# Attention scores for the exponentials from stacks of bfloat16 levels, with the maximum as three more rows and two sets of stacks

## The chip, the cores and the metric

The kernel runs on one core of a Trainium2 chip. The metric is the device time of one execution in microseconds. Engines are called PE (the matrix engine, with PEld for its weight loads), DVE (vector), ACT (scalar), POOL (GpSimd) and SP (it issues DMAs here).

## The reference

Four layers on x of shape (8, 256, 32, 32) in float32: an attention block with an MLP, a deformable convolution bottleneck, a binary convolution and a DCNv3 block. The change lies in the attention, which for each of 8 images, with N = 1024 pixels and 16 heads of key width 16 and value width 64, computes

```python
y = _bn(xf, g1, b1)
q = (einsum('bcn,oc->bon', y, wq) + bq).reshape(B, NH, KD, N).transpose(0, 1, 3, 2)
k = (einsum('bcn,oc->bon', y, wk) + bk).reshape(B, NH, KD, N)
v = (einsum('bcn,oc->bon', y, wv) + bv).reshape(B, NH, D, N).transpose(0, 1, 3, 2)
attn = softmax(einsum('bhnk,bhkm->bhnm', q, k) / KD ** (-0.5), axis=-1)   # scores times 4
o = einsum('bhnm,bhmd->bhnd', attn, v).transpose(0, 1, 3, 2).reshape(B, NH * D, N)
xf = xf + einsum('bdn,od->bon', o, wp) + bp
```

## The kernel before

**Blocks and steps.** The attention is cut into 32 groups of four heads of one image, and each group into two halves of the queries (512 each): 64 blocks. A block has 8 steps, one for each 128 keys (`kt` 0 to 7); there are 512 steps in all, run as one pipeline by `step(t)`. The order of the instructions of PE, ACT, DVE and POOL is the order in which the program emits them; only SP's queue of DMAs is ordered by the framework.

**What a step does**, in this order:

- `exps` (L443) of the next step: for each of four heads a float32 matmul (L453) of 128 keys by 512 queries into an "sc" bank (four in rotation), then ACT's exponential (L454) into an `e` buffer that holds two heads (six in rotation). The matmul contracts 32 rows: 16 rows of k and q, a row that is 1 in `ks` and minus the query's maximum in `qs`, and zero rows. The four heads lie in four groups of 32 partitions.
- `found(0)`, `attend` of heads 0 and 1, `found(1)`, `attend` of heads 2 and 3, `found(2)`, then planned work in three places (0, 1, 2), then `found(3)`.

`found` calls `score_max` (L399), which looks for the maxima of a block AHEAD = 11 steps before its own step: two bfloat16 matmuls of 64 queries by 512 keys (L408, a pair of heads side by side) into a "pb" bank, and DVE's maximum over it (L412). There are two "pb" banks, and every projection, `total` and `add_projected` uses them in rotation too, so a matmul into one waits until DVE or ACT has read what it held two uses before.

The bfloat16 scores come from *stacks* `sq` and `sk`. q and k are each split in three bfloat16 levels (`split`: L359 subtracts the first level, ACT copies the second at L364, L366 leaves the third; DVE does the subtractions), written to DRAM (`lev_d`), and `stack` (L374) reads them back so that eight products of a level of q and a level of k lie on eight times 16 rows. There is one set of stacks; the next group's are loaded when this group's maxima are found. `spread` (L380) brings the float32 q and k, by way of `u_d` in DRAM, into `qs` and `ks`, of which there are two sets.

`enter_max` (L422), once a block, at `kt` = 5 of the block before it, place 0 (the block's first `exps` come at `kt` = 7): DVE clears and reduces (L430, L431), transposes four 32x32 squares (L434), and SP issues four DMAs (L441), one for each head, into the maximum's row of `qs`.

`attend` (L460) multiplies the exponentials with v (L465, two heads to a pair) and adds them up for the denominators: POOL adds 128x1024 float32 per pair of heads (L473 at `kt` = 1, L475 after), 14 a block. In the last block DVE takes half of them. The denominators are finished during the next block: `total` (PE L486, ACT L493) at its `kt` = 3, `narrow` (four DMAs, L499) at 4, `invert` (DVE, L502) at 6, `put` (L506) at 7, `lay` (four DMAs, L513) at 8, `scale` (POOL, L518, 128x512, twice) at 10 and 11, `add_projected` (PE L548, DVE L554 or L556) at 13 and 15.

Beside this, planned by group: `project_v` (L391) of the next group at four steps of the 16, `project_qk` (L333) for two groups at once in every second group (its steps 8, 9, 10 and 14), each followed by its splits, `stack` in 6 of the 16 steps, and `normed` on ACT. The prologue projects and splits for the first two groups (on POOL) and finds the first block's maxima in float32 (`score_max_first`) from `qs` and `ks`.

Of the kernel before, what the change touches and what calls it, by code (L numbers as in the profile page):

```python
# [8 lines left out]
F32 = mybir.dt.float32  # L9
# [19 lines left out]
DH, HID = NH * HD, 1024  # L29

# [128 lines left out]
def conv_seq_kernel(ctx: ExitStack, tc: tile.TileContext, d: dict, out: bass.AP):  # L159
# [76 lines left out]
    with ExitStack() as s0:  # L236
# [10 lines left out]
        row16 = w.tile([P, 1], F32, name="row16")  # L247
        nc.vector.tensor_add(row16, ident[:, 16:17], ident[:, 48:49])
        nc.vector.tensor_add(row16, row16, ident[:, 80:81])
        nc.vector.tensor_add(row16, row16, ident[:, 112:113])  # L250
        qs = [w.tile([P, N], F32, name=f"q{i}") for i in range(2)]
        ks = [w.tile([P, N], F32, name=f"k{i}") for i in range(2)]
        for i in range(2):
            nc.gpsimd.memset(qs[i], 0.0)
            nc.vector.tensor_copy(ks[i], row16.to_broadcast([P, N]))
        sq, sk = ([w.tile([P, 2, N], BF16, name=f"s{n}{i}") for i in range(2)] for n in "qk")
        ones = w.tile([P, HD], F32, name="ones_a")
# [21 lines left out]
        taken = w.tile([P, 4, KD], F32, name="taken")  # L279
# [39 lines left out]
        parts, u_d, lev_d = {}, {}, {}  # L319
        QK = [(0, 0), (1, 0), (1, 1), (0, 1)]  # L320

        def project_qk(b, g2, i):

            if i == 0:
                u_d[b, g2] = ld.tile([2, P, N], F32, name="u_d")
                lev_d[b, g2] = ld.tile([2, 3, P, N], BF16, name="lev_d")
# [20 lines left out]
            nc.sync.dma_start(u_d[b, g2][which, :, cols], u)  # L347
# [21 lines left out]
        def stack(b, g, pair, i, engines=(nc.sync, nc.sync)):  # L369

            for which, dst, eng in ((0, sq[pair], engines[0]), (1, sk[pair], engines[1])):
                r0 = (g % 2) * 64 + pair * 32
                src = lev_d[b, g // 2][which, i % 3 if which else i // 3, r0 : r0 + 32, :]
                eng.dma_start(dst[i * KD : (i + 1) * KD, :, :], src.rearrange("(j r) c -> r j c", r=KD))  # L374

        def spread(b, g, j, eng=nc.sync):

            for u, dst in zip((u_d[b, g // 2][0], u_d[b, g // 2][1]), (qs[g % 2], ks[g % 2])):
                r0 = (g % 2) * 64 + j * KD
                eng.dma_start(dst[32 * j : 32 * j + KD, :], u[r0 : r0 + KD, :])  # L380
# [16 lines left out]
        maxima = {}  # L397

        def score_max(m, s, i):  # L399
# [7 lines left out]
            for c in range(2):  # L407
                nc.tensor.matmul(  # L408
                    ps[c * 64 : (c + 1) * 64, :], sq[pair][:, c, q0 : q0 + 64],
                    sk[pair][:, c, kh * HALF : (kh + 1) * HALF], start=True, stop=True,  # L410
# [3 lines left out]
        def score_max_first(m, s, j):  # L414

            if m not in maxima:
# [5 lines left out]
                ps, qs[0][r, qt * P : (qt + 1) * P], ks[0][r, kh * HALF : (kh + 1) * HALF], start=True, stop=True  # L422
# [3 lines left out]
        def enter_max(m):  # L426

            b, g, h = m
            nm = sp.tile([P, 32], F32, name="nm")
            nc.vector.memset(nm[:, 16:32], 0.0)  # L430
            nc.vector.tensor_reduce(nm[:, 0:16], maxima.pop(m).rearrange("p a b k -> p (a b) k"), AX.X, ALU.max, negate=True)  # L431
            line = sp.tile([32, P], F32, name="line", bufs=1)
            for i in range(4):
                nc.vector.transpose(line[:, 32 * i : 32 * (i + 1)], nm[32 * i : 32 * (i + 1), :])  # L434
            for j in range(4):
                row = qs[g % 2][32 * j + KD : 32 * j + KD + 1, h * HALF : (h + 1) * HALF]
                if m == blocks[0]:
                    src = line[4 * j : 4 * j + 4, :]
                else:
                    src = line[j // 2 * 8 : j // 2 * 8 + 8, j % 2 * 64 : j % 2 * 64 + 64]  # L440
                nc.sync.dma_start(row.rearrange("o (q p) -> o q p", p=src.shape[1]), src)  # L441
# [3 lines left out]
        def exps(m, kt, j):  # L445

            b, g, h = m
            q, k = qs[g % 2], ks[g % 2]
# [3 lines left out]
            r = slice(32 * j, 32 * j + 32)  # L452
# [1432 lines left out]
```

## Time and profile before

| | |
|---|---|
| time, median of 3 executions | 4497.62 us (4492.69 to 4501.10) |
| profiled execution: span | 4474.0 us (its own time beside the span is not given) |
| the three executions less that span | 18.7 to 27.1 us |
| PE busy | 4012.0 us, 90% |
| POOL busy | 3317.7 us, 74% |
| DVE busy | 2858.2 us, 64% |
| ACT busy | 1876.2 us, 42% |
| L412, maxima on DVE | 2016 instructions, 688 ns mean |
| L475 and L473, adds on POOL | 762 and 127, 2423 and 2406 ns mean |
| L453, L465, L408 on PE | 590.7, 1048.4 and 765.7 us busy |
| L359 and L366, splits on DVE | 60 each, 1505 and 1231 ns mean |

The span runs from the first instruction to the last. The page divides it into 40 equal slices and gives a busy share in tenths for each engine and slice; PEclk is the clock that PE was granted, in tenths of full speed. The attention takes slices 1 to 23. Groups of instructions are listed as line, engine, operation, output<-inputs, shape and count; a line of a timeline begins with its start in microseconds and its duration, and ends with the idle time of its engine before it and what ended that. Matmuls are pipelined, so the busy time of a line with several can hold more than the distance of their starts; distances are taken from starts.

### The profile page before, as it was taken

What the parts mean: (1) busy time and instruction counts of PE and PEld (TensorE: products, weight loads), DVE (VectorE), ACT (ScalarE), POOL (GpSimd) and SP (SyncE); (2) the same over time, 40 slices, a digit from 0 to 9 for tenths busy, and PEclk for the clock granted to TensorE, in tenths of its full rate; (3) what the DMA queues carried; (4) which work ended last, traced back from release to release, by engine and by line L of the source; (5) the groups of instructions that cost most, each with busy time, mean ns of one, the idle gap of its engine ahead of it and who ended that gap; (6) DMA issues with size and microseconds to landing.
All of it is one profiled execution on the core that took longest, in us unless ns stands there. A gap on an engine that the chain in (4) does not pass through costs nothing.

```text
span 4474.0 us, 59867 instructions
## 1 busy us (share of the span) xinstructions
PE 4012.0 (90%) x20901; PEld 1525.3 (34%) x20901; DVE 2858.2 (64%) x4976; ACT 1876.2 (42%) x3366; POOL 3317.7 (74%) x2019
## 2 busy tenths in 40 slices
PE   6999999999999999999999998677767766999877
PEld 3333333333333333333333333233223322444332
DVE  5666666666666666666667663455445545688885
ACT  2555555555555555555555542122212212534331
POOL 3889989889889988898888963455454553078887
PEclk8999999999999999999999998888888888999988
DMA  5222222222222222122222112222232332100000
GB/s 165 67 66 55 63 76 57 62 69 60 62 72 57 57 69 70 52 65 74 60 62 69 49 50 60 78 85 85 77 97 67 91 112 63 38 10 15 15 19 21
DMA packets 224279, 284.12 MB, mean 64 GB/s; under 512 B 104400, under 2 KB 134624, under 8 KB 223712
## 3 DMA queue, kind: packets, MB, share of 16 engines
q1 hardware_dynamic: 193408, 196.49, 15.5%
q0 software_dynamic: 28720, 77.90, 5.9%
q10 hardware_dynamic: 1840, 5.81, 0.3%
q8 instruction: 168, 2.75, 0.3%
q14 instruction: 143, 1.17, 0.1%
HBM read 214.10 MB, written 64.34 MB: 62 GB/s over the span
## 4 chain that ended last, share of the span: by engine, by line
PE 74%; DVE 8%; another core or an unknown queue 6%; POOL 5%; issue 4%; ACT 1%; DMA 1%; ACTq 0%; DVEq 0%; SPq 0%; POOLq 0%
PE av L465 19%; PE sc L453 12%; PE pb L408 11%; PE pb L391 5%; PE pb L548 5%; PE pc L1305 3%; PE pm L779 3%; PE po L792 3%; PE pb L333 2%; POOL part L1504 2%; DVE near_p L956 2%; PE pc L1027 1%; DVE samp L960 1%; PE pw L1478 1%
## 5 line engine op out<-in xcount | busy, mean ns | idle before, releaser
L412 DVE TENSOR_REDUCE pm<-pb 128x1 f32<-128x512 f32 x2016 | 1373.7, 688 | 765.7 <-PE pb L408 762.1
L475 POOL TENSOR_TENSOR esum<-esum,e 128x1024 f32<-128x1024 f32 x762 | 1821.0, 2423 | 49.6 <-ACT e L454 49.0
L454 ACT ACTIVATE e<-sc 128x512 f32<-128x512 f32 x2048 | 1056.9, 602 | 593.3 <-PE sc L453 586.9
L465 PE MATMUL av<-e,v 128*64 128x512 f32 x4096 | 1048.4, 592 | 0.0
L934 POOL DMA_INDIRECT g<-table,idx x576 | 549.8, 955 | 560.6 <-DVE near_p L956 287.6
L408 PE MATMUL pb<-sk,sq 128*64 128x512 bf16 x4032 | 765.7, 386 | 13.4 <-DVE pm L412 11.8
L453 PE MATMUL sc<-q,k 32*128 32x512 f32 x4096 | 590.7, 639 | 0.0
L408 PEld LDWEIGHTS <-sq 128*64 128x64 bf16 x4032 | 246.2, 109 | 854.6 <-issue 841.0
L473 POOL TENSOR_TENSOR esum<-e 128x1024 f32<-128x1024 f32 x127 | 303.1, 2406 | 244.4 <-ACT e L454 244.4
L465 PEld LDWEIGHTS av<-e,v 128*64 128x64 f32 x4096 | 287.4, 137 | 234.7 <-issue 140.6
L1504 POOL TENSOR_TENSOR part<-part,pr 128x512 f32<-128x512 f32 x212 | 276.1, 1302 | 54.6 <-DVE pr L1487 43.3
L792 PE MATMUL po<-hid,kept 128*128 128x512 f32 x512 | 253.7, 646 | 54.1 <-DVE x L796 46.6
L1487 DVE TENSOR_TENSOR pr<-pw,v 128x512 f32<-128x512 f32 x394 | 253.9, 682 | 59.2 <-POOL part L1504 31.8
L1305 PE MATMUL pc<-xpad,kept 128*128 128x512 f32 x576 | 276.4, 604 | 11.3 <-DMA bom<-in_l_bom 8.0
L779 PE MATMUL pm<-y,wide 128*128 128x512 f32 x512 | 245.3, 626 | 30.3 <-ACT hid L784 22.4
L548 PE MATMUL pb<-o,wp 128*64 128x512 f32 x1024 | 243.0, 594 | 1.6 <-DVE r L526 1.1
L391 PE MATMUL pb<-wide,y 128*64 128x256 f32 x2048 | 244.1, 381 | 0.4 <-DVE pm L412 0.4
L453 PEld LDWEIGHTS sc<-q,k 32*128 32x128 f32 x4096 | 164.9, 183 | 231.2 <-issue 184.7
L784 ACT ACTIVATE hid<-pm,vec 128x512 f32<-128x512 f32 x128 | 86.9, 686 | 271.7 <-PE pm L779 137.4
L395 ACT COPY v<-pb 128x512 f32<-128x512 f32 x128 | 75.0, 586 | 291.9 <-PE pb L391 291.9
L956 DVE TENSOR_TENSOR near_p<-g,near_p 128x320 f32<-128x320 f32 (+1 forms) x384 | 177.3, 462 | 13.2
L960 DVE TENSOR_TENSOR samp<-samp,near_p 128x320 f32<-128x320 f32 (+1 forms) x384 | 174.0, 453 | 13.2
(266 smaller groups left out, 3903.7 us busy)
## 6 DMA issues: line engine op xcount, KB each, us to landing
sq<-lev_d SPq DMA_DIRECT2D x512, 64.0 KB
r<-inv_d SPq DMA_DIRECT2D x252, 128.0 KB
sk<-lev_d SPq DMA_DIRECT2D x496, 64.0 KB
lev_d<-lev SPq DMA_DIRECT2D x180, 128.0 KB
u_d<-u SPq DMA_DIRECT2D x60, 256.0 KB
g<-table,idx POOLq DMA_INDIRECT x576
out<-res SPq DMA_DIRECT2D x32, 256.0 KB
q<-u_d SPq DMA_DIRECT2D x124, 64.0 KB
```

Of the source, the lines that this page charges most:

```text
L391: nc.tensor.matmul(ps[c * 64 : (c + 1) * 64, (mt % 2) * 256 : (mt % 2 + 1) * 256], ys[b][:, t, k0 : k0 + 64], wv[:, t, g * 256 : (g + 1) * ...
L408: nc.tensor.matmul(ps[c * 64 : (c + 1) * 64, :], sq[pair][:, c, q0 : q0 + 64], sk[pair][:, c, kh * HALF : (kh + 1) * HALF], start=True, st ...
L412: nc.vector.tensor_reduce(maxima[m][:, pair, qt, kh : kh + 1], ps, AX.X, ALU.max)
L453: nc.tensor.matmul(ps, k[r, kt * P : (kt + 1) * P], q[r, h * HALF : (h + 1) * HALF], start=True, stop=True)
L454: nc.scalar.activation(es[m, kt, j // 2][:, j % 2, :], ps, AF.Exp)
L465: nc.tensor.matmul(av[i * HD : (i + 1) * HD, :], vss[b, g][:, kt, j * HD : (j + 1) * HD], e[:, i, :], start=kt == 0, stop=kt == NT - 1,)
L475: eng.tensor_add(sums[m, pair], sums[m, pair], es.pop((m, kt, pair)))
L548: nc.tensor.matmul(ps[c * 64 : (c + 1) * 64, :], wp[:, 2 * g + i, o0 : o0 + 64], outs[(b, g, h), i], start=i == 0, stop=i == 1,)
L779: nc.tensor.matmul(ps, w1[:, t, i * P : (i + 1) * P], ys[b, h][:, t, :], start=t == 0, stop=t == 1)
L792: nc.tensor.matmul(pss["o", b, h, t], w2[:, j, t * P : (t + 1) * P], hids[b, h, j], start=j == 0, stop=j == 7)
L934: nc.gpsimd.indirect_dma_start(out=g[:, k, :], out_offset=None, in_=tables[b][:TR, :], in_offset=bass.IndirectOffsetOnAxis(ap=idxs[b][:, t ...
L1305: nc.tensor.matmul(S["c", b, h], wc[:, t, k, :], tap(xpads[t], k, H // 2, h * H // 2), start=t == k == 0, stop=t == 1 and k == 8,)
```

## The change

Four things change in the attention.

- The eighth product leaves the stacks (`PRODUCTS` = 7, 112 rows). Rows 112 to 114 of `sq` hold minus the maximum in three bfloat16 levels, against rows of ones in `sk`. There are two sets of stacks. `exps` multiplies the stacks: for each head two bfloat16 matmuls of 64 keys by 512 queries with 115 rows. `qs`, `ks`, `row16`, `u_d` and `spread` go; the first block's float32 q and k lie in two `e` buffers.
- `enter_max` splits the maxima on DVE (reduce, copy, subtract, copy, subtract, on 128x16), transposes eight 32x32 squares in bfloat16, and issues 12 DMAs on SP, of 8x64 bfloat16 each. The zeros of the unused columns of `levels` are set once.
- The two adds of `kt` = 1 move from POOL to DVE.
- AHEAD is 12, so that `enter_max` comes at `kt` = 4; splits of two of the four `project_qk` come one step earlier; stacks are loaded at steps 0, 1 and 2 (and 4, 5, 6) of a group, where it was 1, 2 and 3 (and 5, 6, 7).

```diff
...
 DH, HID = NH * HD, 1024
+PRODUCTS = 7
+TERMS = PRODUCTS * KD
...
-        row16 = w.tile([P, 1], F32, name="row16")
-        nc.vector.tensor_add(row16, ident[:, 16:17], ident[:, 48:49])
-        nc.vector.tensor_add(row16, row16, ident[:, 80:81])
-        nc.vector.tensor_add(row16, row16, ident[:, 112:113])
-        qs = [w.tile([P, N], F32, name=f"q{i}") for i in range(2)]
-        ks = [w.tile([P, N], F32, name=f"k{i}") for i in range(2)]
+        sq, sk = ([[w.tile([P, 2, N], BF16, name=f"s{n}{i}{j}") for j in range(2)] for i in range(2)] for n in "qk")
         for i in range(2):
-            nc.gpsimd.memset(qs[i], 0.0)
-            nc.vector.tensor_copy(ks[i], row16.to_broadcast([P, N]))
-        sq, sk = ([w.tile([P, 2, N], BF16, name=f"s{n}{i}") for i in range(2)] for n in "qk")
-        ones = w.tile([P, HD], F32, name="ones_a")
+            for j in range(2):
+                (nc.gpsimd if j else nc.vector).memset(sk[i][j], 1.0)
+        ones = w.tile([P, 32], F32, name="ones_a")
         nc.vector.memset(ones, 1.0)
...
                 nc.scalar.copy(dst[:, t, :].rearrange("p (n r) -> p n r", r=KD), src)
-        taken = w.tile([P, 4, KD], F32, name="taken")
+        taken = ep.tile([P, 2, HALF], F32, name="e")[:, 0, 0 : 4 * KD].rearrange("p (n r) -> p n r", r=KD)
         nc.gpsimd.tensor_copy(taken, ident.rearrange("p (n r) -> p n r", r=32)[:, :, 0:KD])
...
-        parts, u_d, lev_d = {}, {}, {}
+        parts, lev_d, first_qk = {}, {}, {}
         QK = [(0, 0), (1, 0), (1, 1), (0, 1)]
...
             if i == 0:
-                u_d[b, g2] = ld.tile([2, P, N], F32, name="u_d")
                 lev_d[b, g2] = ld.tile([2, 3, P, N], BF16, name="lev_d")
...
             nc.scalar.activation(u, ps, AF.Identity, bias=bias[:, g2 : g2 + 1], scale=scale)
-            nc.sync.dma_start(u_d[b, g2][which, :, cols], u)
             nc.scalar.copy(lev[0], u)
...
-            for which, dst, eng in ((0, sq[pair], engines[0]), (1, sk[pair], engines[1])):
+            for which, dst, eng in ((0, sq[g % 2][pair], engines[0]), (1, sk[g % 2][pair], engines[1])):
                 r0 = (g % 2) * 64 + pair * 32
...
                 eng.dma_start(dst[i * KD : (i + 1) * KD, :, :], src.rearrange("(j r) c -> r j c", r=KD))
-        def spread(b, g, j, eng=nc.sync):
-            for u, dst in zip((u_d[b, g // 2][0], u_d[b, g // 2][1]), (qs[g % 2], ks[g % 2])):
-                r0 = (g % 2) * 64 + j * KD
-                eng.dma_start(dst[32 * j : 32 * j + KD, :], u[r0 : r0 + KD, :])
...
         maxima = {}
+        levels = w.tile([P, 2, 32], BF16, name="levels")
+        nc.vector.memset(levels, 0.0)
...
                 nc.tensor.matmul(
-                    ps[c * 64 : (c + 1) * 64, :], sq[pair][:, c, q0 : q0 + 64],
-                    sk[pair][:, c, kh * HALF : (kh + 1) * HALF], start=True, stop=True,
+                    ps[c * 64 : (c + 1) * 64, :], sq[g % 2][pair][:TERMS, c, q0 : q0 + 64],
+                    sk[g % 2][pair][:TERMS, c, kh * HALF : (kh + 1) * HALF], start=True, stop=True,
                 )
...
             nc.tensor.matmul(
-                ps, qs[0][r, qt * P : (qt + 1) * P], ks[0][r, kh * HALF : (kh + 1) * HALF], start=True, stop=True
+                ps, first_qk[0][r, qt * P : (qt + 1) * P], first_qk[1][r, kh * HALF : (kh + 1) * HALF], start=True, stop=True
             )
...
             b, g, h = m
-            nm = sp.tile([P, 32], F32, name="nm")
-            nc.vector.memset(nm[:, 16:32], 0.0)
-            nc.vector.tensor_reduce(nm[:, 0:16], maxima.pop(m).rearrange("p a b k -> p (a b) k"), AX.X, ALU.max, negate=True)
-            line = sp.tile([32, P], F32, name="line", bufs=1)
-            for i in range(4):
-                nc.vector.transpose(line[:, 32 * i : 32 * (i + 1)], nm[32 * i : 32 * (i + 1), :])
+            nm = sp.tile([P, 2, NT], F32, name="nm")
+            nc.vector.tensor_reduce(nm.rearrange("p a b -> p (a b)"), maxima.pop(m).rearrange("p a b k -> p (a b) k"), AX.X, ALU.max, negate=True)
+            for i in range(2):
+                nc.vector.tensor_copy(levels[:, :, 8 * i : 8 * i + 8], nm)
+                nc.vector.tensor_sub(nm if i == 0 else levels[:, :, 16:24], nm, levels[:, :, 8 * i : 8 * i + 8])
+            line = sp.tile([32, 2, P], BF16, name="line", bufs=1)
+            for pair in range(2):
+                for i in range(4):
+                    nc.vector.transpose(line[:, pair, 32 * i : 32 * (i + 1)], levels[32 * i : 32 * (i + 1), pair, :])
             for j in range(4):
-                row = qs[g % 2][32 * j + KD : 32 * j + KD + 1, h * HALF : (h + 1) * HALF]
-                if m == blocks[0]:
-                    src = line[4 * j : 4 * j + 4, :]
-                else:
-                    src = line[j // 2 * 8 : j // 2 * 8 + 8, j % 2 * 64 : j % 2 * 64 + 64]
-                nc.sync.dma_start(row.rearrange("o (q p) -> o q p", p=src.shape[1]), src)
+                for l in range(3):
+                    if m == blocks[0]:
+                        src = line[8 * l + j % 2 * 4 : 8 * l + j % 2 * 4 + 4, j // 2, :]
+                    else:
+                        src = line[8 * l : 8 * l + 8, j // 2, j % 2 * 64 : j % 2 * 64 + 64]
+                    row = sq[g % 2][j // 2][TERMS + l : TERMS + l + 1, j % 2, h * HALF : (h + 1) * HALF]
+                    nc.sync.dma_start(row.rearrange("o (q p) -> o q p", p=src.shape[1]), src)
...
             b, g, h = m
-            q, k = qs[g % 2], ks[g % 2]
+            q, k = sq[g % 2][j // 2], sk[g % 2][j // 2]
             if j % 2 == 0:
...
             ps = ps_s.tile([P, HALF], F32, name="sc")
-            r = slice(32 * j, 32 * j + 32)
-            nc.tensor.matmul(ps, k[r, kt * P : (kt + 1) * P], q[r, h * HALF : (h + 1) * HALF], start=True, stop=True)
+            for c in range(2):
+                k0 = kt * P + c * 64
+                nc.tensor.matmul(
+                    ps[c * 64 : (c + 1) * 64, :], k[: TERMS + 3, j % 2, k0 : k0 + 64],
+                    q[: TERMS + 3, j % 2, h * HALF : (h + 1) * HALF], start=True, stop=True,
+                )
             nc.scalar.activation(es[m, kt, j // 2][:, j % 2, :], ps, AF.Exp)
...
-            eng = nc.vector if m == blocks[-1] and pair else nc.gpsimd
+            eng = nc.vector if kt == 1 or (m == blocks[-1] and pair) else nc.gpsimd
             if kt == 1:
...
             for j in range(4):
-                nc.tensor.matmul(ps[32 * j : 32 * j + 32, :], ones[:, 0:32], sums[m, j // 2][:, j % 2, :], start=True, stop=True)
+                nc.tensor.matmul(ps[32 * j : 32 * j + 32, :], ones, sums[m, j // 2][:, j % 2, :], start=True, stop=True)
             return ps
...
         steps = NT * nblk
-        AHEAD = NT + 3
+        AHEAD = NT + 4
...
                     plan(t0 + (0, 1, 2, late)[i], 1, project_v, *nxt, i)
-                    plan(t0 + 9 + i, 0, spread, *nxt, i)
                 for pair in range(2):
-                    for i in range(8):
-                        plan(t0 + (1, 1, 2, 2, 2, 3, 3, 3)[i] + 4 * pair, 2, stack, *nxt, pair, i)
+                    for i in range(PRODUCTS):
+                        plan(t0 + (0, 0, 1, 1, 1, 2, 2)[i] + 4 * pair, 2, stack, *nxt, pair, i)
                 if nxt == groups[-1]:
...
                     plan(t0 + (8, 9, 10, 14)[i], 1, project_qk, b_, g2, i)
-                    at = t0 + (9, 11, 14, 17)[i]
+                    at = t0 + (9, 11, 14, 16)[i]
                     plan(at, 0, split, b_, g2, i, 0)
                     plan(at, 2, split, b_, g2, i, 1)
-                    plan(t0 + (10, 12, 16, 18)[i], 0, split, b_, g2, i, 2)
+                    plan(t0 + (10, 12, 15, 17)[i], 0, split, b_, g2, i, 2)
         for n, m in enumerate(blocks):
...
                 bias(t)
+            for i in range(2):
+                first_qk[i] = ep.tile([P, 2, HALF], F32, name="e").rearrange("p a c -> p (a c)")
             for i in range(4):
...
                 for j in range(4):
-                    dst = (qs, ks)[which][0][32 * j : 32 * j + KD, h * HALF : (h + 1) * HALF]
+                    dst = first_qk[which][32 * j : 32 * j + KD, h * HALF : (h + 1) * HALF]
                     (nc.gpsimd if j % 2 else nc.sync).dma_start(dst, parts[i][0][j * KD : (j + 1) * KD, :])
...
             for pair in range(2):
-                for i in range(8):
+                for i in range(PRODUCTS):
                     stack(0, 0, pair, i, (nc.sync, nc.gpsimd))
```

## The prediction

> **What bounds the kernel now.** I read the page first: busy time by engine, the 40 slices, the chain that ended last.
>
> ```profile
> PE 4012.0 (90%) x20901; PEld 1525.3 (34%) x20901; DVE 2858.2 (64%) x4976; ACT 1876.2 (42%) x3366; POOL 3317.7 (74%) x2019
> ...
> PE   6999999999999999999999998677767766999877
> ...
> PEclk8999999999999999999999998888888888999988
> ...
> PE 74%; DVE 8%; another core or an unknown queue 6%; POOL 5%; issue 4%; ACT 1%; DMA 1%; ACTq 0%; DVEq 0%; SPq 0%; POOLq 0%
> ```
>
> The attention is slices 1 to 23, with PE at 9 tenths or more at full clock. A window inside it (columns: PE, PEld, DVE, ACT, POOL busy, granted clock, DMA share, GB/s):
>
> ```profile
> 1500.00:2000.00 500.00, 497.19 (x3188) 177.33 (x3184) 332.13 (x536) 268.45 (x505) 446.69 (x201) 1.00 0.22 62
> ```
>
> PE waits for nothing (497 of 500 us), and POOL, at 89%, is next. So a PE saving counts in full, and anything that makes PE wait does too. One step on PE, from the timeline of its instructions (start, duration):
>
> ```profile
> 1507.13 1.14 PE L453 MATMUL sc<-q,k 32*128 32x512 f32 x8
> 1508.20 0.41 PE L408 MATMUL pb<-sk,sq 128*64 128x512 bf16 x2
> 1508.44 1.02 PE L465 MATMUL av<-e,v 128*64 128x512 f32 x4
> 1509.30 0.38 PE L408 MATMUL pb<-sk,sq 128*64 128x512 bf16 x2
> 1509.51 1.02 PE L465 MATMUL av<-e,v 128*64 128x512 f32 x4
> ```
>
> By starts, a bfloat16 pair costs 0.21 to 0.24 us (I use 0.215), an av pair 0.86, the scores 1.07 plus 0.12 lost around their change of form, say 1.195. A step with nothing else lasts 3.77 (1503.36 to 1507.13); a block of 8 steps 40.24 (its first maxima DMA at 1520.73, that of 8 blocks later at 1842.69).
>
> The second view is the timeline of DVE and POOL. Where DVE needs SBUF for two inputs while POOL adds, it waits for POOL's whole instruction:
>
> ```profile
> 1752.89 2.73 DVE L359 TENSOR_TENSOR u<-u,lev 128x512 f32<-128x512 f32 x1
> 1755.55 1.87 DVE L412 TENSOR_REDUCE pm<-pb 128x1 f32<-128x512 f32 x3
> ...
> 1593.01 2.73 DVE L359 TENSOR_TENSOR u<-u,lev 128x512 f32<-128x512 f32 x1
> 1596.39 0.41 PE L408 MATMUL pb<-sk,sq 128*64 128x512 bf16 x2 [0.43 <-DVE pm L412]
> ```
>
> The shortest L359 is 0.70, so 2.0 us are wait; it ends when one of POOL's adds (2.33 each, back to back) ends. Three reduces are then due, and in the second case PE waits 0.43. Some single-input copies wait too: under a POOL memset of 3822.04 to 3824.4,
>
> ```profile
> 3823.51 0.96 DVE L1224 CAST identb<-ident 128x128 bf16<-128x128 f32 x1
> 3824.51 0.17 DVE L1276 COPY spread<-group 128x12 f32<-128x12 f32 x1
> ```
>
> the first ended with the memset; the second, with an outer dimension of 3, began under POOL's next memset and did not wait. L412, the transposes L434 and adds with one input in PSUM (L556, 692 ns throughout) do not wait either.
>
> **The change, per block of 8 steps.**
>
> *Scores.* Eight bfloat16 matmuls in four pairs, 4 x 0.215 = 0.86 for 1.195: −0.335 a step, −2.7 a block, 171 us over 512 steps. Contracting 112 or 115 rows for 128 changes nothing: a pair's time is its 512 columns.
>
> *enter_max.* On DVE now: reduce 0.2, four transposes of 0.215, 1.1 us in all, at kt=5. Then: reduce 0.2, copy, subtract, copy, subtract, each waiting for the one before (0.20 start to start, from the prologue's 128x2 arithmetic at L217), eight transposes of 0.215: 0.2+0.8+1.7 = 2.7 with no waits. The subtractions have two inputs in SBUF. The copies have one, f32 to bfloat16 like L1224, with an outer dimension of 2. POOL has queued adds here (two of 2.33 a step, for which steps of 3.4 have no room), so I let all four wait: the first meets a running add half way, 1.2; each time DVE lets go, POOL's next add starts and the next small instruction waits for all of it, 2.2. Such turns are seen in the last block, where both engines add: DVE's adds take 2.1 to 3.2 there, and POOL's L518 2.25 for 1.27. 1.2+3x2.2 = 7.8, stretch 10.5.
>
> Bounds for one small instruction: 0.2 (L1276's row, no wait) and 2.33+0.2 (one whole add). L359 and L1224 are nearest.
>
> Behind enter_max on DVE stand the reduces of found(3) and of the next step. found(1) of kt=5 needs the "pb" bank that found(3)'s reduce frees, and PE gets there 1.94 after found(3)'s pair has ended (scores 0.86, found(0) 0.215, av 0.86). PE's wait: found(2)'s reduce, still running, 0.63 + 10.5 + 0.62 + 0.1 − 1.94 = 9.9; where project_v lies at kt=4 (two blocks of eight) 8.2; mean 9.5. That is the largest term.
>
> *Moved adds.* At kt=1 two 128x1024 adds leave POOL for DVE. Alone one costs about 1.15 (estimate from L359's 0.70 for 512 columns). The first finds POOL mostly idle, the second waits for POOL's first add of kt=2: with four reduces 2.48+2x1.15+1.8 = 6.6 against PE's 5.17 (3.44 + project_v or the like, 1.73); with a split in half of the blocks, 0.6+1.8 more. Mean +2.4. Bounds 0 (no wait, the reduces' slack covers it) and +4.
>
> *Splits.* Already waiting (means 1.51 and 1.23); with fuller DVE queues +0.7.
>
> *DMAs.* 12 lines for 4 on SP's queue, 0.70 each as L441 issues now: 8.5 for 2.8, landing some 1.2 later. enter_max is one step earlier. What waits in that queue: narrow's four DMAs, the stacks of the next group (in half of the blocks ten of them stand behind the lines), and in one block of four narrow itself is behind the lines, with DVE's invert behind it (about 2). The last head's scores come two steps after PE's wait has ended, 11.2+3.2+3.4+0.7 = 18.5 us after enter_max began (1.7 more where kt=6 holds a projection); the last line is there at 10.5+8.5+1.2 = 20.2, an earlier head's 2.1 sooner: a wait of 0 to 1.7, say 0.7. Mean, with narrow's 2 in one block of four, +1.2; bounds 0 and +3.
>
> *Clock.* PE idled 5.75 us before the MLP, and then:
>
> ```profile
> 2650.00:2655.00 5.00, 0.27 (x1) 0.30 (x2) 4.46 (x9) 0.32 (x2) 4.31 (x3) 0.78 1.01 393
> 2655.00:2660.00 5.00, 5.00 (x7) 2.08 (x7) 1.38 (x4) 0.69 (x1) 0.00 (x0) 0.54 0.36 82
> 2660.00:2665.00 5.00, 5.00 (x13) 2.13 (x13) 0.85 (x2) 2.07 (x4) 0.00 (x0) 1.00 0.30 74
> ```
>
> About 4.3 us at half speed, 2.1 lost. A gap of 9.5 in each block would do the same; part is absorbed where PE then waits anyway: +1.5.
>
> *At nothing.* u_d and spread DMAs go, a product fewer: SP issues 76 in a group of two blocks (28 stacks, 24 lines, 24 others) where it issued 74 (32, 8, 34), and SP is no bound. POOL's two adds fewer (4.8 us) free an engine that PE does not wait for. The moved splits and stacks keep their order against what they feed. The prologue's memsets lie beside its loads; its longer stacks' chain and 12 lines cost some 4 us once.
>
> **Sum.** −2.7+9.5+2.4+0.7+1.2+1.5 = +12.6 a block; 63 blocks (the first block's maxima come in the prologue) 794, plus 4: 798. The profiled execution has a span of 4474.0; its own time is not on the page, but all three runs lie 18.7 to 27.1 us above that span, so the sum stands against the median, 4497.6: 5296 us.
>
> **Two rules of the Trainium skill.** "SBUF — State Buffer", section "SBUF: two separate sides", has VectorE and GpSimd share a port pair under an exclusive lock, held for the whole instruction; "VectorE: DVE Perf Modes", section "What auto-detection actually checks", lets a single-input instruction take the two-port mode if the outermost dimensions in and out are both even or equal. By that the copies (2 x 8) wait like L1224; counting only instructions with two inputs, +7.6 a block would be the sum. "TensorE: Matmul & The Clock Gate", Part 1, gives a half clock until about 3.4 us of busy time: by it 1.7 a gap for the 2.1 that the row shows.
>
> **Rivals.** *B, only the subtractions wait* (the copies pass like L1276): stretch 2.7+1.2+2.2 = 6.1, PE's wait 5.5, mean 5.1, clock 0.9: +7.6, 4498+479+4 = 4981; up to 5060. *C, POOL's queue is dry at kt=4*, since PE's own waits let it catch up, and one wait or none is left: stretch 2.7 to 5, PE's wait 1.7 to 4.0, adds, splits and lines as above, little from the clock: +3.3 to +5.9, 4710 to 4874. *F, faster*: POOL, at 12 adds a block, leaves DVE alone at both places, transposes of half the bytes take half the time, and lines issue like stacks (0.47), in time. A stretch of 1.9 costs PE 1.3 less what project_v hides, and with adds and splits between nothing and 1.1 a block −0.6 to −2.7 is left: 4460 to 4327. It turns where PE's waits together come to 2.7 us a block, little more than one add of POOL's. For it speaks that L359's fastest instruction waited for nothing; against it the mean of 1505 ns and POOL's 89%. That the scores don't get cheaper is excluded by the L408 rows, the same form.
>
> **How the numbers follow.** A (four waits, 5100 to 5430) 0.58; B 0.15; C 0.13; F 0.10; no change 0.04. 0.2%, 9 us, is about what a measurement tells from no change. Range 4700 to 5430: it holds A, B and C; F, no change and what lies above are left out. Faster 0.10, same 0.04, slower 0.86; of A and B alone the range would be 4980 to 5430.
>
> **What would show it.** Score pairs L449 at 0.215, 0.86 a step; copies L423 and subtractions L424 with means near 2 us (0.2: F); PE's wait at L399 near 10 us once a block, for DVE; the block at 52 to 53 us; granted clock below 1.00 in the attention. I am wrong if POOL's adds do not run when enter_max does, or if the lock goes to DVE twice in a row.

## The result, and the profile after

The changed kernel takes 5264.4 us (median of four executions, 5261.4 to 5270.2) where the kernel before takes 4497.2: a ratio of 1.172, 95% interval 1.170 to 1.174. The forecast was 5296 us. The profiled execution took 5270.2 us, with a span of 5268.3.

The page of the changed kernel: busy time, PE and its clock in 40 slices, the chain that ended last by engine.

```profile
PE 4037.7 (77%) x20901; PEld 1811.2 (34%) x20901; DVE 3677.0 (70%) x5549; ACT 1863.4 (35%) x3366; POOL 3005.7 (57%) x1890
...
PE   6777787777777777777777777787676776699887
...
PEclk8989898989998989899989899898888887899988
...
PE 48%; DVE 29%; issue 7%; another core or an unknown queue 5%; POOL 5%; SPq 2%; ACT 2%; DMA 2%; DVEq 0%; POOLq 0%; ACTq 0%
```

PE is no longer the bound. In the attention, now slices 1 to 26, its share is 7 tenths, its clock dips all the way through, and DVE's share of the chain has gone from 8% to 29%. The loss is all in the attention: the MLP's first matmul (L779) starts at 3427.1 us, where it started at 2654.7. The distance is 772 us. Between the maxima's first and last reduction in `enter_max` a block takes 52.08 us, where it took 39.97: +12.1.

The same window as before, then the groups of it that count (busy, mean ns, idle time before them and what ended it):

```profile
1500.00:2000.00 500.00, 388.55 (x2484) 181.97 (x2485) 377.25 (x499) 203.50 (x387) 295.48 (x136) 0.92 0.13 36
```

```profile
L403 DVE TENSOR_REDUCE pm<-pb 128x1 f32<-128x512 f32 x312 | 209.4, 684 | 92.0 <-PE pb L399 90.6
...
L399 PE MATMUL pb<-sk,sq 112*64 112x512 bf16 x620 | 126.3, 396 | 107.9 <-DVE pm L403 102.4 <-ACT u L342 2.2 <-DMA inv_d<-r 1.7
...
L472 DVE TENSOR_TENSOR esum<-e 128x1024 f32<-128x1024 f32 x20 | 42.7, 2136 | 0.0
...
L423 DVE CAST levels<-nm 128x16 bf16<-128x16 f32 x19 | 35.2, 1853 | 0.7
...
L424 DVE TENSOR_TENSOR nm<-nm,levels 128x16 f32<-128x16 f32 x9 | 20.4, 2265 | 0.3
L424 DVE TENSOR_TENSOR levels<-nm,levels 128x16 bf16<-128x16 f32 x9 | 16.2, 1798 | 0.3
L428 DVE STREAM_TRANSPOSE line<-levels 32x32 bf16<-32x32 bf16 x72 | 14.4, 200 | 2.0 <-DVE levels L424 0.4
```

The maxima's matmul L399 waits 107.9 us in these 500, of which 102.4 were ended by DVE's reduce. Instructions on 16 numbers a partition take 1.8 to 2.3 us each. One `enter_max` on DVE and POOL, in order of time, with the PE wait it ends in:

```profile
1570.32 18.55 POOL L474 TENSOR_TENSOR esum<-esum,e 128x1024 f32<-128x1024 f32 x8
...
1580.12 0.17 DVE L421 TENSOR_REDUCE nm<-pm 128x16 f32<-128x32 f32 x1
1580.34 1.65 DVE L423 CAST levels<-nm 128x16 bf16<-128x16 f32 x1
1582.02 2.28 DVE L424 TENSOR_TENSOR nm<-nm,levels 128x16 f32<-128x16 f32 x1
1584.33 2.26 DVE L423 CAST levels<-nm 128x16 bf16<-128x16 f32 x1
1586.63 2.26 DVE L424 TENSOR_TENSOR levels<-nm,levels 128x16 bf16<-128x16 f32 x1
1588.93 1.75 DVE L428 STREAM_TRANSPOSE line<-levels 32x32 bf16<-32x32 bf16 x8
1590.61 2.06 DVE L403 TENSOR_REDUCE pm<-pb 128x1 f32<-128x512 f32 x3
...
1591.30 0.64 PE L399 MATMUL pb<-sk,sq 112*64 112x512 bf16 x2 [7.94 <-DVE pm L403]
```

POOL has eight adds in a row from 1570.32 to 1588.87. The reduce takes 0.17 beside them; the copy waits for the rest of one add, and the next three for a whole add each, the last until POOL's row of adds ends. Here project_v lies at `kt` = 4, which hides a part of the wait. From the reduce to the last transpose 10.6 us pass (forecast: 10.5), and PE waits 7.94. Then the clock (columns as above; the last but two is the granted clock):

```profile
1590.00:1592.00 2.00, 0.70 (x4) 0.51 (x5) 1.81 (x7) 0.00 (x0) 0.00 (x0) 0.50 0.01 1
1592.00:1594.00 2.00, 2.00 (x8) 0.69 (x6) 0.67 (x1) 0.00 (x0) 0.00 (x0) 0.50 0.02 2
1594.00:1596.00 2.00, 2.00 (x9) 0.59 (x7) 0.69 (x1) 0.00 (x0) 0.00 (x0) 0.61 0.02 2
1596.00:1598.00 2.00, 2.00 (x18) 1.19 (x16) 1.35 (x3) 0.87 (x2) 0.00 (x0) 1.00 0.02 2
```

PE starts again at 1591.3 and works at half speed to about 1595.6.

### The profile page after: what moved, and what is told of

Its sections match the earlier page's. It is cut to its first block, busy times and chain, and to the rows that moved or that the text cites. A ratio compares the mean times of both kernels' runs of the same rounds, so it can differ in the third digit from the quotient of the medians.

```text
span 5268.3 us, 60558 instructions
## 1 busy us (share of the span) xinstructions
PE 4037.7 (77%) x20901; PEld 1811.2 (34%) x20901; DVE 3677.0 (70%) x5549; ACT 1863.4 (35%) x3366; POOL 3005.7 (57%) x1890
## 4 chain that ended last, share of the span: by engine, by line
PE 48%; DVE 29%; issue 7%; another core or an unknown queue 5%; POOL 5%; SPq 2%; ACT 2%; DMA 2%; DVEq 0%; POOLq 0%; ACTq 0%
PE av L464 13%; PE pb L399 8%; PE sc L449 5%; DVE levels L423 5%; PE pb L547 4%; DVE esum L472 4%; DVE pm L403 4%; PE pc L1305 3%; DVE nm L424 3%; PE pm L779 2%; PE pb L380 2%; DVE levels L424 2%; DVE line L428 2%; PE po L792 2%
## 5 line engine op out<-in xcount | busy, mean ns | idle before, releaser
L399 PE MATMUL pb<-sk,sq 112*64 112x512 bf16 x4032 | 826.0, 398 | 732.2 <-DVE pm L403 699.3
L464 PE MATMUL av<-e,v 128*64 128x512 f32 x4096 | 1130.1, 622 | 0.0
L399 PEld LDWEIGHTS <-sq 112*64 112x64 bf16 x4032 | 323.6, 111 | 1332.0 <-issue 1280.9
L449 PE MATMUL sc<-sq,sk 115*64 115x512 bf16 x4096 | 539.7, 379 | 8.5 <-DMA sq<-line 8.4
L464 PEld LDWEIGHTS av<-e,v 128*64 128x64 f32 x4096 | 340.9, 142 | 197.1 <-issue 101.9
L449 PEld LDWEIGHTS <-sk 115*64 115x64 bf16 x4096 | 269.2, 110 | 207.1 <-issue 69.6
L547 PE MATMUL pb<-o,wp 128*64 128x512 f32 x1024 | 297.3, 702 | 1.2 <-DVE r L525 1.0
L779 PE MATMUL pm<-y,wide 128*128 128x512 f32 x512 | 248.9, 633 | 33.6 <-ACT hid L784 26.0
L472 DVE TENSOR_TENSOR esum<-e 128x1024 f32<-128x1024 f32 x128 | 271.6, 2123 | 1.0 <-ACT e L453 1.0
L423 DVE CAST levels<-nm 128x16 bf16<-128x16 f32 x128 | 238.5, 1864 | 4.4
L380 PEld LDWEIGHTS pb<-wide,y 128*64 128x64 f32 x2048 | 150.0, 137 | 130.9 <-DVE pm L403 81.9
```

What stands on the lines that cost most here:

```text
L380: nc.tensor.matmul(ps[c * 64 : (c + 1) * 64, (mt % 2) * 256 : (mt % 2 + 1) * 256], ys[b][:, t, k0 : k0 + 64], wv[:, t, g * 256 : (g + 1) * ...
L399: nc.tensor.matmul(ps[c * 64 : (c + 1) * 64, :], sq[g % 2][pair][:TERMS, c, q0 : q0 + 64], sk[g % 2][pair][:TERMS, c, kh * HALF : (kh + 1) ...
L423: nc.vector.tensor_copy(levels[:, :, 8 * i : 8 * i + 8], nm)
L449: nc.tensor.matmul(ps[c * 64 : (c + 1) * 64, :], k[: TERMS + 3, j % 2, k0 : k0 + 64], q[: TERMS + 3, j % 2, h * HALF : (h + 1) * HALF], st ...
L464: nc.tensor.matmul(av[i * HD : (i + 1) * HD, :], vss[b, g][:, kt, j * HD : (j + 1) * HD], e[:, i, :], start=kt == 0, stop=kt == NT - 1,)
L472: eng.tensor_add(sums[m, pair], es.pop((m, 0, pair)), es.pop((m, 1, pair)))
```

## The experiments

The theory: the two copies and two subtractions of `enter_max` each wait for an add of POOL's, PE waits for the reduces behind them, and loses clock after it. The rivals: the adds moved to DVE cost more; the twelve line DMAs are late; small DVE instructions on this layout are slow whatever POOL does.

The runs were made on several chips. On one, below called the second chip, the kernel before takes 4146 us; on the others it takes 4497 to 4501. The difference lies behind the attention: from the MLP's first matmul to the end 1819 us pass in the profile of the kernel before, and 1489 us on the second chip in the profile of the same kernel with its adds moved. So times are set against the kernel before on the same chip; between chips the start of the MLP is compared.

### Levels by reductions

```diff
-            nm = sp.tile([P, 2, NT], F32, name="nm")
-            nc.vector.tensor_reduce(nm.rearrange("p a b -> p (a b)"), maxima.pop(m).rearrange("p a b k -> p (a b) k"), AX.X, ALU.max, negate=True)
+            nm = sp.tile([P, 2, 2, NT, 2], F32, name="nm")
+            top = maxima.pop(m).rearrange("p a b k -> p (a b) k").rearrange("p (a b) k -> p a b k", a=2)
+            nc.vector.tensor_reduce(nm[:, 0, :, :, 0], top, AX.X, ALU.max, negate=True)
+            nc.vector.tensor_reduce(levels[:, :, 0:8], top, AX.X, ALU.max, negate=True)
             for i in range(2):
-                nc.vector.tensor_copy(levels[:, :, 8 * i : 8 * i + 8], nm)
-                nc.vector.tensor_sub(nm if i == 0 else levels[:, :, 16:24], nm, levels[:, :, 8 * i : 8 * i + 8])
+                l = levels[:, :, 8 * i : 8 * i + 8]
+                nc.vector.tensor_reduce(nm[:, i, :, :, 1], l.rearrange("p a (b k) -> p a b k", k=1), AX.X, ALU.max, negate=True)
+                if i == 0:
+                    nc.vector.tensor_reduce(nm[:, 1, :, :, 0], nm[:, 0], AX.X, ALU.add)
+                with nc.allow_low_precision(reason="levels of bfloat16"):
+                    nc.vector.tensor_reduce(levels[:, :, 8 * i + 8 : 8 * i + 16], nm[:, i], AX.X, ALU.add)
```

> The changed kernel, with the maxima's three levels made by seven reductions on DVE (a maximum over one element for the sign, a sum over two for the difference) in place of a reduction, two copies and two subtractions. Theory (the copies and subtractions wait for POOL's adds; reductions do not, as L421 with 171 to 186 ns throughout): each of the seven takes about 0.2 us, DVE's stretch in enter_max falls from 10.3 to about 3.2, PE's wait at kt=5 from 9.1 to about 2, the granted clock in the attention returns from 0.92 to near 1.00; 4620 to 4760 us. Rival 1 (the moved adds of kt=1 hold PE up) and rival 2 (the 12 lines are late): enter_max is not what PE waits for in the end, 5150 to 5264 us.

Measured: 4802.8 us, before 4500.6, ratio 1.067 (1.065 to 1.069). The theory's direction and most of its size: 462 us of the loss go, and the time lies 43 us above the range. One `enter_max` of this kernel on DVE:

```profile
1517.68 0.18 DVE L422 TENSOR_REDUCE nm<-pm 128x16 f32<-128x32 f32 x1
1517.78 0.18 DVE L423 TENSOR_REDUCE levels<-pm 128x16 bf16<-128x32 f32 x1
1517.99 0.17 DVE L426 TENSOR_REDUCE nm<-levels 128x16 f32<-128x16 bf16 x1
1518.20 0.19 DVE L428 TENSOR_REDUCE nm<-nm 128x16 f32<-128x32 f32 x1
...
1518.99 1.75 DVE L434 STREAM_TRANSPOSE line<-levels 32x32 bf16<-32x32 bf16 x8
...
1521.36 0.41 PE L399 MATMUL pb<-sk,sq 112*64 112x512 bf16 x2 [2.17 <-DVE pm L403]
```

Seven reductions take 1.2 us beside POOL's adds, which run throughout. PE's wait is 2.2 to 2.4 in six blocks of eight (4.1 and 0.6 in the other two), and the granted clock from 1521 to 1525 is 0.60: here a wait of 2.2 us cost up to another 1.6 in clock. The expectation had the clock back near 1.00.

### The adds back on POOL

```diff
-            eng = nc.vector if kt == 1 or (m == blocks[-1] and pair) else nc.gpsimd
+            eng = nc.vector if m == blocks[-1] and pair else nc.gpsimd
```

> The changed kernel with the two adds of kt=1 back on POOL, the rest as changed. Theory: enter_max keeps its four waits, POOL having more to add; what goes is PE's wait of 2.0 us at kt=1 in each block and some waits of splits: minus 60 to minus 190 us, 5075 to 5205 us. Rival 1 (the moved adds are the main loss): below 4800 us. A third case: POOL, fuller, lengthens waits elsewhere as much, 5264 +- 30.

Measured: 5108.1 us, before 4500.6, ratio 1.135 (1.134 to 1.137). That is 156 us less than the changed kernel, 2.5 a block, inside the theory's range; the waits at `enter_max` stay (mean 9.2 us over 18 waits above 3 us between 1400 and 2300 us; 9.0 over 17 in the changed kernel). So the moved adds are a loss, and the smaller one.

### POOL quiet

```diff
             elif kt > 1:
-                eng.tensor_add(sums[m, pair], sums[m, pair], es.pop((m, kt, pair)))
+                e = es.pop((m, kt, pair))
+                if eng is nc.vector or kt not in (3, 4, 5, 6):
+                    eng.tensor_add(sums[m, pair], sums[m, pair], e)
```

> The changed kernel with POOL's adds of kt 3 to 6 left out (the denominators miss four of the eight key blocks, so the output is not the reference's); enter_max and everything else as changed. Theory: with no add of POOL's running, copies and subtractions take 0.2 us each, PE's wait at kt=5 falls from 9.1 to about 1.5, and the time to 4480 to 4700 us. If the small instructions are slow by themselves (2 us each whatever POOL does), the time stays above 5150 us.

Measured: 4724.9 us (one execution), 25 above the range; before 4500.6. The copies and subtractions, the same instructions as in the changed kernel:

```profile
L423 DVE CAST levels<-nm 128x16 bf16<-128x16 f32 x22 | 3.8, 174 | 0.8
...
L424 DVE TENSOR_TENSOR nm<-nm,levels 128x16 f32<-128x16 f32 x11 | 1.9, 175 | 0.4
L424 DVE TENSOR_TENSOR levels<-nm,levels 128x16 bf16<-128x16 f32 x11 | 1.9, 175 | 0.4
```

174 and 175 ns: they are not slow by themselves. PE's wait behind `enter_max` is 1.9 to 3.0 us in six blocks of eight and not the 1.5 expected; the moved adds still cost 2.0 (1.63 and 0.36) in each block.

### The four instructions in the kernel before

```diff
+            spare = sp.tile([P, 2, NT], F32, name="spare")
+            nc.vector.tensor_copy(levels[:, :, 0:8], nm[:, 0:16].rearrange("p (a b) -> p a b", a=2))
+            nc.vector.tensor_sub(spare, nm[:, 0:16].rearrange("p (a b) -> p a b", a=2), levels[:, :, 0:8])
+            nc.vector.tensor_copy(levels[:, :, 8:16], spare)
+            nc.vector.tensor_sub(levels[:, :, 16:24], spare, levels[:, :, 8:16])
             line = sp.tile([32, P], F32, name="line", bufs=1)
```

> The kernel before with the two copies and two subtractions added to its enter_max (written to tiles that nothing reads), nothing else changed. Theory: they wait for POOL's adds as in the changed kernel, so PE waits 6 to 9 us in each block and loses clock after it: 4497 + 63 x (7 to 12) = 4940 to 5250 us. If the loss belongs to another part of the change: 4500 to 4560 us.

Measured: 5098.6 us (one execution), before 4500.6: +598, 9.5 us a block, from four instructions of 16 columns whose results nothing reads. In its trace they follow POOL in turns, as in the changed kernel:

```profile
1550.42 11.99 POOL L481 TENSOR_TENSOR esum<-esum,e 128x1024 f32<-128x1024 f32 x5
...
1554.02 1.54 DVE L434 CAST levels<-nm 128x16 bf16<-128x16 f32 x1
...
1555.59 2.26 DVE L435 TENSOR_TENSOR spare<-nm,levels 128x16 f32<-128x16 f32 x1
1557.89 2.26 DVE L436 CAST levels<-spare 128x16 bf16<-128x16 f32 x1
1560.19 2.26 DVE L437 TENSOR_TENSOR levels<-spare,levels 128x16 bf16<-128x16 f32 x1
...
1564.00 0.64 PE L409 MATMUL pb<-sk,sq 128*64 128x512 bf16 x2 [7.82 <-DVE x L562]
```

Where POOL runs out of adds, the wait ends: in another block an add of POOL's ends at 1510.73, the two instructions behind it take 0.17 us each, and PE waits 2.54.

These four alone account for most of the change's loss, without any of its other parts. The four runs settle the main question: PE's waits of 8 to 10 us go with POOL quiet, and with reductions in place of these four instructions, and such waits come with these four alone.

### The moved adds in the kernel before

```diff
-            eng = nc.vector if m == blocks[-1] and pair else nc.gpsimd
+            eng = nc.vector if kt == 1 or (m == blocks[-1] and pair) else nc.gpsimd
```

> The kernel before with its two adds of kt=1 on DVE, nothing else changed. Theory: the second add, perhaps both, waits for an add of POOL's, and PE for the reduces behind them, 2.0 us a block as in the changed kernel, up to 4.5 where POOL is behind: 4620 to 4780 us. Rival (the moved adds relieve POOL and cost PE nothing): 4480 to 4510 us.

Measured: 4318.5 us, before 4146.0 on this chip, ratio 1.042 (1.040 to 1.043): +172.5, 2.7 a block. The expectation's microseconds were written for the other chip; its loss of 123 to 283 holds. PE waits 0.37 and 1.63 us at `kt` = 1, as in the changed kernel.

### Four line DMAs

In all blocks but the first:

```diff
-                for l in range(3):
...
-                        src = line[8 * l : 8 * l + 8, j // 2, j % 2 * 64 : j % 2 * 64 + 64]
-                    row = sq[g % 2][j // 2][TERMS + l : TERMS + l + 1, j % 2, h * HALF : (h + 1) * HALF]
-                    nc.sync.dma_start(row.rearrange("o (q p) -> o q p", p=src.shape[1]), src)
...
+                    src = line[0:24, j // 2, j % 2 * 64 : j % 2 * 64 + 64]
+                    rows_ = sq[g % 2][j // 2][TERMS : TERMS + 3, j % 2, h * HALF : (h + 1) * HALF]
+                    nc.sync.dma_start(rows_.rearrange("o (q p) -> o q p", p=64), src)
```

> The changed kernel with four line DMAs of 24 rows (three rows of the stack each) in place of twelve of 8. Theory: SP's queue delays nothing that PE waits for, but narrow and invert a little: 5235 to 5270 us. Rival (the twelve DMAs are a main cause): below 5150 us.

Measured: 4884.6 us against 4146.0, ratio 1.178 (1.176 to 1.180), on the second chip. The MLP starts at 3390.4 us, 36.7 before the changed kernel's: 0.6 a block. The DMAs are a small part, a little more than the theory's 30.

### Reductions, and the adds back

The two edits above together.

> The changed kernel with the levels by reductions and the two adds of kt=1 back on POOL. Theory: against the kernel with reductions alone (4803) PE's 2.0 us at kt=1 go in each block: 4640 to 4700 us; the wait at enter_max (2.2 us and the clock after it) stays. Rival: POOL, 14 adds and two scalings (36.6 us) in a block of 42, is the bound or makes splits wait as much: 4740 to 4810 us.

Measured: 4254.6 us against 4146.0, ratio 1.026 (1.025 to 1.028). The MLP starts at 2756.0, 208 us before that of reductions alone (2963.9): 3.3 a block where 2.0 was expected, and beyond the 103 to 163 us of its range. Between 1500 and 2000 us PE's idle time falls from 5.3 to 2.8 a block (59.4 of 500 in blocks of 44.9; 33.6 in blocks of 41.5), its busy time from 39.6 to 38.7, with the granted clock up from 0.97 to 0.98. The 14 adds on POOL are not the bound: POOL is busy 429 of 500 us.

### Everything spread out

Reductions and four line DMAs as above, and:

```diff
+        def enter_lines(m):
...
             line = sp.tile([32, 2, P], BF16, name="line", bufs=1)
...
-            elif kt > 1:
-                eng.tensor_add(sums[m, pair], sums[m, pair], es.pop((m, kt, pair)))
+            elif kt > 1 and not (kt == 2 and pair == 0 and eng is nc.gpsimd and m != blocks[-1]):
+                for p in (1, 0) if kt == 2 and m != blocks[-1] else (pair,):
+                    eng.tensor_add(sums[m, p], sums[m, p], es.pop((m, kt, p)))
...
             plan(t1_ - AHEAD, 0, enter_max, m)
+            plan(t1_ - AHEAD + 1, 0, enter_lines, m)
```

> The changed kernel with each of the found waits taken away: the levels by reductions on DVE (1.3 us at kt=4), the transposes and lines one step later (1.75 us at kt=5), four line DMAs of 24 rows in place of twelve, and POOL's two adds of kt=2 in the other order, so that POOL starts when DVE's second add of kt=1 is done. Theory: no wait of PE's above 0.5 us is left except at splits (0.7 a block) and the full clock holds; the gain at the scores shows: 4497 - 170 + 63 x (0.7 to 1.5) = 4370 to 4430 us. Rival (the score matmuls of 115 rows or the longer chain of DMAs take the gain back by themselves): 4490 to 4650 us.

Measured: 4145.2 us against 4146.0, ratio 0.9998 (0.9989 to 1.0007): no difference. The expectation's gain of 67 to 127 us was missed. The swap worked: DVE's adds of kt=1 take 1214 ns now, where they took 2136. The number lies in the rival's range, but neither of its causes is there: the pairs of score matmuls still start 0.215 apart, and between the first block and the last no scores wait for lines. PE waits in the window of 500 us for 22.3 us in all, and in one block of eight, where a split stands just ahead of the reductions and waits for POOL, PE waits 2.58 us, here with half clock behind it (so after six of the seven such waits). In the other blocks with a split there, one of eight too, project_v hides most of it, and PE waits 0.83:

```profile
1599.16 2.31 DVE L361 TENSOR_TENSOR lev<-u,lev 128x512 bf16<-128x512 f32 x1
...
1603.25 0.64 PE L399 MATMUL pb<-sk,sq 112*64 112x512 bf16 x2 [2.58 <-DVE pm L403]
```

### Two heads at a time, and splits moved

The first pair of heads has its maxima four steps before the second. Here `enter_max(m, pair)` and `enter_lines(m, pair)` do one pair:

```diff
-            plan(t1_ - AHEAD, 0, enter_max, m)
-            plan(t1_ - AHEAD + 1, 0, enter_lines, m)
+            for pair in range(2):
+                early = 0 if pair or m == blocks[0] else 4
+                plan(t1_ - AHEAD - early, 0, enter_max, m, pair)
+                plan(t1_ - AHEAD - early + (2 if early else 1), 0, enter_lines, m, pair)
```

> The kernel with the waits spread out (the last of these that equalled the kernel before), with enter_max done for two heads at a time: the first pair's maxima are complete four steps earlier, so its reductions go to kt=0 and its transposes and lines to kt=2, and only the second pair's are left at kt=4 and kt=5. Theory: what is left of PE's waits at kt=5 and kt=6 (0.35 each in a block) goes with the second pair's four transposes alone: 20 to 50 us less than the kernel before. Rival: waits only move to kt=0 and kt=2, where a projection's reads share the banks: no change within 10 us.

Measured: 4477.9 us against 4497.4 on one of the other chips, ratio 0.996 (0.994 to 0.997): 19.5 us less than the kernel before, just short of the 20 to 50 expected.

The last run moves the projection and the splits besides:

```diff
-                    plan(t0 + (8, 9, 10, 14)[i], 1, project_qk, b_, g2, i)
-                    at = t0 + (9, 11, 14, 16)[i]
+                    plan(t0 + (8, 9, 12, 14)[i], 1, project_qk, b_, g2, i)
+                    at = t0 + (9, 11, 15, 17)[i]
...
-                    plan(t0 + (10, 12, 15, 17)[i], 0, split, b_, g2, i, 2)
+                    plan(t0 + (10, 14, 16, 18)[i], 0, split, b_, g2, i, 2)
```

> The same in pairs, and the splits moved off kt=4: the third projection of q and k from a group's step 10 to 12, the first subtractions to steps 9, 11, 15, 17 and the second ones to 10, 14, 16, 18. Theory: the wait of 2.6 us that a split ahead of enter_max gives in one block of four, with the half clock after it (about 4 us together), goes: 16 blocks x 4 = 64 us more, so 60 to 115 us less than the kernel before (ratio 0.972 to 0.986). Rival: a split waits for an add of POOL's wherever it stands, and PE with it: no more than 30 us better than the kernel in pairs.

Measured: 4476.0 us, ratio 0.995 (0.993 to 0.997), no different from the kernel in pairs. The rival's case holds: the wait of 2.5 us is gone from its place (one of 2.6 stands elsewhere in the run), and waits of 1.1 and 0.8 us stand at the splits' new places, each in about one block of four. The theory also counted too much: in the kernel in pairs the wait of 2.5 us comes in one block of eight, seven times in all, and the clock fell after three of them, so some 20 us were to be had (an estimate from these waits) and not 64. The two versions in pairs lie 0.4 to 0.5% under the kernel before, clear of the noise but small; the next section says where the rest of the 171 us of the scores stays.

## Why the prediction was right

**Scores, −2.7 a block.** The pair takes 0.215 and four of them 0.86 in the changed kernel (the scores of a step start at 1516.33 and those of the next at 1519.79: 3.46, forecast 3.44). The contraction's 112 or 115 rows for 128 make no difference. Not all of it was kept, though. In the version in pairs, between 1400 and 1960 us, steps with a projection of v last 5.35 us in the median with the listed waits taken off, 5.19 at the least; in the kernel before 5.50 both times. So about half of the 0.31 is gone there. It is taken here for waits too short to be listed, which no row shows by themselves: a matmul's recorded end lies some 0.2 after the next one's start, and would hide them.

**`enter_max`, +9.5.** The waits of PE between 1400 and 2300 us run from 7.9 to 10.05, 9.0 in the mean. In 47 of the 63 blocks all four instructions wait: over the whole run the copies take 2128 ns in the median of 128 (174 at least), the subtractions 2262. That the copies wait too was chosen from L1224's row, and it decided between the forecast and the rival of two waits (4981). In the other 16 POOL's row of adds had ended, and the last subtraction takes 0.175 us, so rival C's dry queue came true in one block of four, for the last of the four waits. PE's wait was no shorter there (8.3 to 10.05 between 1400 and 2300 us): in those blocks a split ahead of `enter_max` waits for POOL as well:

```profile
1634.02 1.94 DVE L361 TENSOR_TENSOR lev<-u,lev 128x512 bf16<-128x512 f32 x1
...
1642.81 0.18 DVE L424 TENSOR_TENSOR levels<-nm,levels 128x16 bf16<-128x16 f32 x1
...
1645.56 0.64 PE L399 MATMUL pb<-sk,sq 112*64 112x512 bf16 x2 [10.03 <-DVE pm L403]
```

That the four wait beside POOL's adds and not without them agrees with the Trainium skill, "SBUF — State Buffer", section "SBUF: two separate sides", an exclusive lock held for the whole instruction, and with "VectorE: DVE Perf Modes", section "What auto-detection actually checks", by which the 2 x 8 copies take the two-port mode.

**Moved adds, +2.4.** 2.0 of wait in each block (0.36 and 1.63), 2.5 by taking them back, 2.7 by putting them into the kernel before. The first add met an idle POOL and took 1.22, the second waited for POOL's first add of `kt` = 2, as the step said:

```profile
1510.68 1.22 DVE L472 TENSOR_TENSOR esum<-e 128x1024 f32<-128x1024 f32 x1
...
1512.04 2.35 POOL L474 TENSOR_TENSOR esum<-esum,e 128x1024 f32<-128x1024 f32 x1 [11.30 <-DVE esum L472]
1512.41 3.05 DVE L472 TENSOR_TENSOR esum<-e 128x1024 f32<-128x1024 f32 x1
...
1516.12 0.41 PE L399 MATMUL pb<-sk,sq 112*64 112x512 bf16 x2 [1.62 <-DVE pm L403]
```

The step's own parts, 6.6−5.17 and 2.4 in half of the blocks, add up to +2.6 and not +2.4.

**Lines, +1.2: too high.** The scores' matmul L449 waited 8.4 us for lines in the whole run, all of it in the last block, where 0.7 a block was put down. Four DMAs for twelve bring 0.6.

**Clock, +1.5: too low.** Over 32 whole blocks in the middle of the attention PE is busy 40.3 us a block in the changed kernel (1289.21 of 1676.34 us). The version in pairs, at a granted clock of 1.00, does the same matmuls in 38.2 (1223.43 of 1276.23). So about 2.1 are lost to the clock, if waits too short to be listed are alike in both. The step put the loss after one gap at 2.1 and had 0.6 of it hidden; little is hidden. Its rows of the gap before the MLP were read a little short: they give 4.9 us at half speed (0.27 in the first row, 4.6 in the second), a loss of 2.4.

**Sum.** In the same blocks PE is idle 12.1 a block, for 0.2 before (1281.51 busy of 1287.93). PE was to be busy 40.05−2.7 = 37.35 a block; the 0.9 from there to 38.2 are the waits too short to be listed, as said above, which the forecast had not. −2.7+0.9+11.9+2.1 = +12.2 for 52.39−40.25 = +12.1 measured there, and +12.6 forecast. With 9.0 at `enter_max` and 2.0 at the moved adds, 0.9 of the 11.9 are left for splits and lines, where the forecast had 1.9. The forecast's waits together (9.5+2.4+0.7+1.2 = 13.8) were 1.9 too high, its clock and short waits (1.5 for 3.0) 1.5 too low. So the mechanism and the largest term were right, and that the total came within 0.5 a block is in part luck: the misses cancel. The version in pairs, by the same sum: −2.7+0.9+1.4 (idle 1.65 for 0.2) = −0.4, for 39.88 against 40.25.

**The rival of a faster kernel** fell with L423 and L424. Its turning point, 2.7 us of waits a block, is where the experiments ended: reductions, spread work and pairs bring them to 2.3 above what was there before, 1.4 of idle time and the 0.9 of short waits.

## What to carry to other kernels

Before an instruction is put on VectorE between others that a tight pipeline waits for, look whether GpSimd has adds queued there: here such copies and two-input instructions on SBUF cost GpSimd's instruction time (2.26 us) and not their own (0.17), each time anew in a dependent chain. Price an instruction by its longest row beside the other engine, not by its shortest. Reductions did the same work here without the wait, and adds with one operand in PSUM (L555, at most 693 ns in the changed kernel) did not wait either.

## What was not expected

A wait of 2 us can halve PE's clock. Between 1400 and 2300 us of nine of the runs, with PE's waits of 1.3 us and more and the granted clock in the 3 us after them: none of 92 waits up to 1.93 us was followed by a lower clock (below 0.95); of 50 waits from 1.95 to 2.7 us 30 were (the shortest 1.96, and one of 2.58 was not); all 57 from 3 us up were. In the two other runs of the changed kernel's kind the same holds: after 17 waits of 1.6 us the clock stayed, after 17 from 7.9 us up it fell, and after one of 2.62 it stayed. "TensorE: Matmul & The Clock Gate", Part 1, of the Trainium skill gives an idle window of about 3.4 us; here some waits of less than two thirds of it were enough. What decides between 1.95 and 2.7 was not looked into.
